# The residual add of a recurrent layer's feed-forward result: VectorE or GpSimd, and where a factor of one half is applied

## The chip, the cores and the metric

The kernel runs on one core of a Trainium2 chip. The metric is the device time of one execution in microseconds (us), taken as the median of several runs. Each engine works through its own queue in order: TensorE (PE, with its weight loads as PEld), VectorE (DVE), ScalarE (ACT), GpSimd (POOL) and SyncE (SP), which issues most of the transfers.

## The reference, cut to what matters

Four layers follow one another on an activation of 32 sequences x 64 positions x 256 features: a cross-attention layer (L0), two transformer blocks with self-attention, cross-attention and an MLP (L1, L2), and a recurrent layer (L3) in the manner of RWKV. The change is in the last lines of L3, its feed-forward part:

```python
x = x + att * g @ Wo.T
xn2 = _ln(x, ln2_w, ln2_b)
sx2 = _token_shift(xn2, state[:, i0])
xk = xn2 + sx2 * ffn_maa_k
xr = xn2 + sx2 * ffn_maa_r
rr = jax.nn.sigmoid(xr @ ffn_Wr.T)
kk = jnp.square(jax.nn.relu(xk @ ffn_Wk.T))
x = x + rr * (kk @ ffn_Wv.T)
return x
```

The sigmoid is computed as (1 + tanh(z / 2)) / 2. So the result is x + 0.5 * (1 + tanh) * (kk @ ffn_Wv.T), and the factor of one half can stand in the last step or in the weights ffn_Wv.

## The kernel before

The 2048 rows are held in SBUF in four groups (`xg[g]`, 128 partitions x 4 x 256). The recurrent layer works on eight slabs of 256 rows (`n` = 0 to 7; slab n is half u = n % 2 of group g = n // 2). For each slab `recurrent` returns three lists of small pieces:

- first: a layer norm (`norm`), the token-shift mixes (`mixed`, L681, VectorE, two inputs in SBUF; `mix`, which evacuates px on VectorE in L718 and adds xn on GpSimd in L721), the projections to receptance, key, value and gate (pr, pk, pv, pg), and the decay.
- second: `spread` (L754, a transfer that copies the values of a slab out of DRAM to 128 partitions), `outer` and `read` (L814, VectorE products of 128x2048), `scan` (L829, VectorE), `over_keys`, the group norm (L847 to L866) and the output projection with Wo (pwo, L875), which is added to x in L216.
- third: the second layer norm, the mixes xk and xr, and the three feed-forward products. `done_r` puts the tanh into the tile rr (ScalarE, L909). `done_v` finishes the slab: L914 computes (rr + 1) * pfv with pfv in PSUM, L915 multiplies by 0.5 and adds the rows of x, and L916 sends the result to DRAM through SP.

Each piece has a due time (FIRST, SECOND and THIRD plus the slab's number; ENDS shifts the last slabs), and `emit` writes all pieces out in the order of these times. The eight slabs therefore overlap: while slab n finishes, slabs n + 3 and n + 4 are in their second and first lists, and the rest of L2's MLP is interleaved with the first slabs. From that order the tile framework works out the final order on each engine when the program is built: among the instructions that its own timing estimate holds to be ready, it takes the one written first. Each engine then runs its queue in order, with semaphore waits for data and for buffers.

The weights of L3 that are needed late (Wg, Wo, ffn_Wk, ffn_Wr, ffn_Wv) are loaded through SP by `load_w` when the pool of the recurrent layer is set up; `ffn_Wv` is a tile of 128 x 2 x 256.

Of the kernel before, what the change touches and what calls it, by code (L numbers as in the profile page):

```python
# [34 lines left out]
ALU = mybir.AluOpType  # L35
# [5 lines left out]
NG = 4  # L41
# [51 lines left out]
def emit(*timed_lists):  # L93
    for _, piece in sorted((p for ps in timed_lists for p in ps), key=lambda p: p[0]):
        piece()
# [3 lines left out]
def tile_xattn_stack(ctx: ExitStack, tc: tile.TileContext, a: dict, out: bass.AP):  # L99
    nc = tc.nc  # L100
# [18 lines left out]
    xg = [const.tile([P, NT, E], FP, name=f"x{g}") for g in range(NG)]  # L119
# [11 lines left out]
    def vec(name, i=0):  # L131
        c = VEC[name] + i
        return vecs[:, c : c + 1]
# [89 lines left out]
    def ring(pool, name, shape, n, fill):  # L223

        tiles = [pool.tile(shape, FP, name=f"{name}{i}", bufs=1) for i in range(n)]
        for t in tiles:
            fill(t)
        turn, busy = [0], [False] * n

        def take():  # L230
            turn[0] += 1
            i = turn[0] % n
            assert not busy[i], name
            busy[i] = True

            def done():
                busy[i] = False

            return tiles[i], done

        return take
# [389 lines left out]
    def recurrent(n, pool, c3):  # L631

        g, u = n // 2, n % 2
# [277 lines left out]
        def done_v(ps):  # L911
            js = slice(2 * u, 2 * u + 2)
            rr = st["rr"]
            nc.vector.scalar_tensor_tensor(rr, rr, 1.0, ps, ALU.add, ALU.mult)  # L914
            nc.vector.scalar_tensor_tensor(rr, rr, 0.5, xg[g][:, js, :], ALU.mult, ALU.add)  # L915
            nc.sync.dma_start(out_rows[g][:, js, :], rr)  # L916

        def ff_norm():
# [2 lines left out]
        third = [(0.5, ff_norm), (0.0, ff_mix), (1.7, ff_key)]  # L921
        third += to_rows(lambda: st["xr"], "ffn_Wr", done_r, "fr")
        third += to_rows(lambda: st["kk"], "ffn_Wv", done_v, "fv")
        return first, second, third


    wts, c3 = {}, {}

    def load_to(pool, name, shape, src):
        c3[name] = pool.tile(shape, FP, name=name, bufs=1)  # L930
        nc.sync.dma_start(c3[name], src)
# [207 lines left out]
    with tc.tile_pool(name="r", bufs=2, reuse_waits="tile") as pool:  # L1139
        def load(name, shape, src):  # L1140
            load_to(pool, name, shape, src)

        def load_w(*names):
            for n in names:
                load(n, [P, 2, E], a["w3"][W3[n]].rearrange("(c p) n -> p c n", p=P))

        def hold(tag, bufs=2, shape=None):
            pool.tile(shape or [P, 2, RR], FP, tag=tag, name=f"hold_{tag}", bufs=bufs)

        def shifted_ring(name):  # L1150

            c3[name] = ring(pool, name, [P, 2, RB, S], 2, lambda t: nc.gpsimd.memset(t[:, :, :, 0], 0.0))

        hold("fx")
        hold("dfx")
        hold("x5", 3)
        hold("nx", 1)
        shifted_ring("wsh")
        hold("xk")
        hold("xr")  # L1160
        hold("kk")
        hold("x")
        hold("rr", 2, [P, 2, E])
        hold("dx")
        shifted_ring("vsh")
        hold("ta", 1, [P, RR + S])
        hold("vT")
        hold("rT")
        hold("tb", 1, [XM, RR])
        hold("rk", 1)  # L1170
        hold("dT", 1, [64, RR])
        selu = c3["selu"] = pool.tile([P, 2, P], FP, name="selu", bufs=1)
        load_w("Wg", "Wo", "ffn_Wk", "ffn_Wr", "ffn_Wv")
        load("s0", [P, 2, RS, B], a["s0"])
        hold("gt")
        hold("at")
        hold("sq", 1)
        shifted_ring("ksh")
        hold("nfx", 1)
        for c in range(2):  # L1180
            nc.vector.tensor_scalar(selu[:, c], c3["sel"][:, c], vec("L3_faaaa", c), None, ALU.mult)
        gnh = c3["gnh"] = pool.tile([P, 4], FP, name="gnh", bufs=1)
        for i, n in enumerate(("L3_gn_w", "L3_gn_b")):
            nc.vector.tensor_scalar(
                gnh[:, 2 * i : 2 * i + 2], vecs[:, VEC[n] : VEC[n] + 2], 0.5, None, ALU.mult
            )

        plan = [late]
        for n in range(2 * NG):
            for pieces, at, end in zip(recurrent(n, pool, c3), (FIRST, SECOND, THIRD), ENDS):  # L1190
                shift = end[n - 2 * NG] if n >= 2 * NG - len(end) else 0.0
                plan.append([(n + t + shift, piece) for t, (_, piece) in zip(at, pieces, strict=True)])
        emit(*plan)
# [78 lines left out]
```

## Time and profile before

| | us |
|---|---|
| median of 3 runs | 1058.6 |
| lowest and highest run | 1056.49 and 1059.2 |
| the profiled execution | 1057.36 |
| its span on the core | 1055.6 |
| busy: TensorE / VectorE | 963.1 / 741.4 |
| busy: ScalarE / GpSimd | 553.4 / 554.9 |

The span runs from the first to the last instruction that the profile shows; the profiled execution's time contains some 1.8 us more. The granted TensorE clock was 0.974 of full speed in the mean. A row of a timeline gives the start and duration in us, the engine, the line of the kernel, the operation, what it writes and reads, and in brackets how long the engine was idle before it and which instruction ended that. Rows of one kind that follow each other are merged ("x2"), so a duration can be that of several instructions.

### The profile page before, as it was taken

The page shows a single profiled execution, that of the slowest core. Times are in us where ns is not written, and L with a number is a line of the kernel's source. Part 1 is how long each engine was busy: PE and PEld are TensorE (multiplying, and loading weights), DVE is VectorE, ACT ScalarE, POOL GpSimd, SP SyncE. Part 2 cuts the span into 40 slices and gives each one's busy share as a digit, 9 for nine tenths or more (in the row PEclk, how much of TensorE's full clock was granted, in tenths as well). Part 3 has the DMA queues.
Part 4 walks back from the last instruction along what each step waited for, and adds up shares of the span by engine and source line. Part 5 has one row for each costly group of instructions (what it writes and reads, how often), then busy time and mean ns, then how long its engine had stood idle before and what let it go on. Part 6 is the DMA issues. An engine that isn't in the chain of part 4 may idle for free.

```text
span 1055.6 us, 25954 instructions
## 1 busy us (share of the span) xinstructions
PE 963.1 (91%) x10636; PEld 776.0 (74%) x10636; DVE 741.4 (70%) x1415; ACT 553.4 (52%) x1279; POOL 554.9 (53%) x584
## 2 busy tenths in 40 slices
PE   8999999998999999989999999997979989989757
PEld 4887787776788987967777778875857777666546
DVE  5863778787875646567777865337588786899984
ACT  4744756454466445654554575533545566355244
POOL 4343998798874347578688875130224431243300
PEclk9999999999999999999999999998989999999889
DMA  9300111111101000141101110021321304223401
GB/s 302 112 22 21 42 27 42 42 28 27 32 2 47 1 16 7 58 135 38 41 23 27 27 52 22 11 67 26 92 65 28 90 12 102 70 52 72 100 1 40
DMA packets 45945, 53.36 MB, mean 51 GB/s; under 512 B 16146, under 2 KB 40068, under 8 KB 43780
## 3 DMA queue, kind: packets, MB, share of 16 engines
q1 hardware_dynamic: 40292, 49.60, 17.6%
q10 hardware_dynamic: 5536, 2.12, 0.8%
q8 instruction: 84, 1.38, 0.5%
q14 instruction: 33, 0.27, 0.1%
HBM read 38.83 MB, written 4.21 MB: 41 GB/s over the span
## 4 chain that ended last, share of the span: by engine, by line
PE 43%; DVE 27%; POOL 14%; ACT 7%; issue 3%; DMA 3%; SPq 2%; ACTq 0%; DVEq 0%; POOLq 0%
DVE vb_r L829 7%; PE pf_L2m L205 4%; PE pfo_L1m L205 3%; PE pfo_L2m L613 3%; DVE vb_r L814 3%; POOL s_L2s L481 2%; PE pf_L1m L205 2%; POOL s_L1c L481 2%; POOL s_L2s L485 2%; PE pr L330 2%; SPq L421 2%; DVE x L216 1%; PE pwo_r L875 1%; POOL s_L1c L485 1%; PE pk_r L210 1%
## 5 line engine op out<-in xcount | busy, mean ns | idle before, releaser
L721 POOL TENSOR_TENSOR x_r<-x_r,xn_r 128x512 f32<-128x512 f32 x40 | 60.6, 1530 | 143.1 <-DVE x_r L718 131.8
L829 DVE TENSOR_TENSOR_SCAN vb_r<-wsh,vb_r 128x512 f32<-128x512 f32 x64 | 76.5, 1262 | 14.2 <-ACT wsh L725 14.2
L613 PE MATMUL pfo_L2m<-w_L,hT_L2m 128*128 128x256 f32 x256 | 61.2, 383 | 0.1
L205 PE MATMUL pfo_L1m<-w_L,hT_L1m 128*128 128x256 f32 x384 | 56.0, 292 | 4.7 <-DVE hT_L1m L605 2.1
L205 PE MATMUL pf_L2m<-lnT_L2m,w_L 128*128 128x256 f32 x384 | 55.2, 294 | 2.1 <-ACT hT_L2m L599 2.1
L205 PEld LDWEIGHTS pfo_L1m<-w_L,hT_L1m 128*128 128x128 f32 x384 | 50.5, 195 | 7.8 <-DVE hT_L1m L605 2.9
L205 PEld LDWEIGHTS pf_L2m<-lnT_L2m,w_L 128*128 128x128 f32 x384 | 49.0, 190 | 5.6 <-ACT hT_L2m L599 2.7
L613 PEld LDWEIGHTS pfo_L2m<-w_L,hT_L2m 128*128 128x128 f32 x256 | 47.0, 190 | 7.9 <-issue 1.3
L481 POOL TENSOR_TENSOR s_L2s<-s_L2s,n 128x512 f32<-128x512 f32 x32 | 41.5, 1314 | 20.9 <-DVE s_L2s L476 15.1
L205 PE MATMUL pf_L1m<-lnT_L1m,w_L 128*128 128x256 f32 x384 | 51.6, 287 | 0.1
L481 POOL TENSOR_TENSOR s_L1s<-s_L1s,n 128x512 f32<-128x512 f32 x32 | 40.5, 1282 | 19.7 <-DVE s_L1s L476 19.6
L481 POOL TENSOR_TENSOR s_L1c<-s_L1c,n_L1c 128x512 f32<-128x512 f32 x32 | 41.0, 1302 | 17.0 <-DVE s_L1c L476 16.8
L481 POOL TENSOR_TENSOR s_L2c<-s_L2c,n_L2c 128x512 f32<-128x512 f32 x32 | 40.5, 1286 | 17.6 <-DVE s_L2c L476 17.6
L205 PEld LDWEIGHTS pf_L1m<-lnT_L1m,w_L 128*128 128x128 f32 x384 | 47.8, 191 | 2.0 <-issue 1.2
L605 DVE TENSOR_TENSOR hT_L1m<-hf_L1m,hT_L1m 128x512 fp32r<-128x512 f32 x32 | 29.2, 916 | 24.6 <-POOL hT_L1m L604 24.6
L604 POOL TENSOR_SCALAR hT_L1m<-hf_L1m 128x512 fp32r<-128x512 f32 x32 | 21.4, 671 | 45.6 <-ACT hf_L1m L599 39.6
L599 ACT ACTIVATE hf_L1m<-pf_L1m,b_L 128x256 f32<-128x256 f32 x64 | 26.8, 473 | 29.1 <-PE pf_L1m L205 26.3
L599 ACT ACTIVATE hT_L2m<-pf_L2m,b_L 128x256 f32<-128x256 f32 x64 | 26.6, 472 | 29.0 <-PE pf_L2m L205 28.9
L718 DVE SCALAR_TENSOR_TENSOR x_r<-px_r,vecs,sx_r 128x256 f32<-128x256 f32 x80 | 33.5, 475 | 9.2 <-PE px_r L150 9.2
L300 ACT ACTIVATE att<-pe,nmx 128x256 f32<-128x256 f32 x64 | 29.6, 478 | 19.1 <-DVE nmx L298 16.8
L814 DVE TENSOR_TENSOR vb_r<-vb_r,rT_r 128x2048 f32<-128x2048 f32 x16 | 38.5, 2413 | 0.0
L150 PE MATMUL pa_r<-vb_r,sel 128*32 128x256 f32 x256 | 20.4, 447 | 19.2 <-DVE vb_r L814 19.2
(383 smaller groups left out, 2973.6 us busy)
## 6 DMA issues: line engine op xcount, KB each, us to landing
vb_r<-vd_r SPq DMA_DIRECT2D x16, 1024.0 KB
raw_w_L<-in_L_w_dram SPq DMA_DIRECT2D x3, 1024.0 KB
y<-in_y_dram SPq DMA_DIRECT2D x8, 256.0 KB
x<-in_x_dram SPq DMA_DIRECT2D x8, 256.0 KB
ctxT_L1c<-in_yT_dram SPq DMA_DIRECT2D x4, 512.0 KB
kbd<-kT_L1s SPq DMA_DIRECT2D x64, 32.0 KB
kbd<-kT_L1c SPq DMA_DIRECT2D x64, 32.0 KB
kbd<-kT_L2s SPq DMA_DIRECT2D x64, 32.0 KB
```

What stands on the lines that cost most here:

```text
L205: nc.tensor.matmul(ps, sta[x], mov[y], start=(at == 0), stop=(at == n - 1))
L300: nc.scalar.activation(att[:, 2 * h + c, :], pe[:, c, :], AF.Exp, bias=nmx[:, h, c : c + 1], accum_out=rs[:, h, c : c + 1],)
L481: nc.gpsimd.tensor_tensor(s[:, r], s[:, r], n(j).unsqueeze(1).broadcast_to([P, 8, S]), ALU.add)
L485: nc.gpsimd.tensor_tensor(s[:, r], s[:, r], mx[:, hs].unsqueeze(2).broadcast_to([P, 8, S]), ALU.subtract)
L599: nc.scalar.activation(raw[:, i], ps[:, i], AF.Gelu_apprx_tanh, bias=w()["b1"][:, 2 * f2 + i : 2 * f2 + i + 1])
L604: nc.gpsimd.tensor_scalar(h[:, 0], raw, 1.0, 0.0, ALU.mult, ALU.add)
L605: nc.vector.tensor_tensor(h[:, 1], raw, h[:, 0], ALU.subtract)
L613: nc.tensor.matmul(st["ps"][:, v], st["h"][:, f, rows], w2[:, f], start=(f == 0), stop=(f == 7))
L718: nc.vector.scalar_tensor_tensor(d[:, c], banks[m][:, c], vec("L3_maa_stack", 2 * m + c), sx_("x", c), ALU.add, ALU.mult)
L721: nc.gpsimd.tensor_tensor(d, d, st["x"], ALU.add)
L814: nc.vector.tensor_tensor(v, v, x.unsqueeze(1).broadcast_to([P, 4, 2 * RR]), ALU.mult)
L829: nc.vector.tensor_tensor_scan(v[:, d], flat(st["wsh"]), v[:, d], 0.0, ALU.mult, ALU.add)
```

## The change

The add of the rows (L915) becomes a plain tensor-tensor add without the factor. In slabs 0 to 6 it is issued on GpSimd, in slab 7 on VectorE. The factor of one half goes into the weights ffn_Wv: after they are loaded, one GpSimd instruction multiplies the tile by 0.5 in place. L914 and L916 stay as they are, on VectorE and SP.

```diff
         def done_v(ps):
             js = slice(2 * u, 2 * u + 2)
             rr = st["rr"]
+
             nc.vector.scalar_tensor_tensor(rr, rr, 1.0, ps, ALU.add, ALU.mult)
-            nc.vector.scalar_tensor_tensor(rr, rr, 0.5, xg[g][:, js, :], ALU.mult, ALU.add)
+            (nc.vector if n == 2 * NG - 1 else nc.gpsimd).tensor_tensor(rr, rr, xg[g][:, js, :], ALU.add)
             nc.sync.dma_start(out_rows[g][:, js, :], rr)
...
         load_w("Wg", "Wo", "ffn_Wk", "ffn_Wr", "ffn_Wv")
+        nc.gpsimd.tensor_scalar(c3["ffn_Wv"], c3["ffn_Wv"], 0.5, 0.0, ALU.mult, ALU.add)
         load("s0", [P, 2, RS, B], a["s0"])
```

## The prediction

> **What bounds the kernel now.** I read the page first, then the recurrent part in stages (busy time by window), then the chain of waits in order of time, and last the rows of VectorE and GpSimd around every execution of L915, the line that changes engine.
>
> ```profile
> PE 963.1 (91%) x10636; PEld 776.0 (74%) x10636; DVE 741.4 (70%) x1415; ACT 553.4 (52%) x1279; POOL 554.9 (53%) x584
> ...
> 910.00:950.00 40.00, 33.89 (x211) 25.07 (x210) 35.79 (x52) 22.55 (x44) 17.84 (x13) 0.99 0.33 80
> 950.00:990.00 40.00, 34.94 (x181) 24.15 (x180) 38.79 (x52) 14.67 (x30) 12.51 (x10) 0.88 0.38 89
> 990.00:1033.00 43.00, 29.35 (x168) 21.46 (x167) 36.64 (x52) 19.94 (x37) 5.81 (x7) 0.88 0.11 30
> 1033.00:1056.00 23.00, 16.48 (x81) 13.35 (x79) 9.08 (x20) 8.26 (x16) 1.26 (x4) 0.98 0.10 34
> ```
>
> In a window's row the columns are the window, its length, then the busy time of TensorE, its weight loads, VectorE, ScalarE and GpSimd. Over the whole span TensorE is the fullest. In the stretch where the changed code runs it is another matter: from 910 to 990 VectorE is busy 35.8 and 38.8 of 40 us, GpSimd 17.8 and 12.5. From 1033 on nobody is full: a chain through all engines ends the kernel. The chain of waits agrees: from 896 to 1017 it runs mostly through VectorE's scans (L829) and products (L814), and after that through TensorE.
>
> L915 runs eight times, at 871.63, 894.84, 957.86, 994.28, 1028.05, 1038.67, 1046.49 and 1051.66 (slabs 0 to 7). What follows it on VectorE decides what its removal is worth. Slab 1, then 2, then 3, and what GpSimd does near 2 and 3 (start, duration, engine, line; in brackets the idle time ahead and who ended it):
>
> ```profile
> 894.84 0.69 DVE L915 SCALAR_TENSOR_TENSOR rr_r<-rr_r,x 128x512 f32<-128x512 f32 x1
> 896.41 9.03 DVE L829 TENSOR_TENSOR_SCAN vb_r<-wsh,vb_r 128x512 f32<-128x512 f32 x8 [0.88 <-ACT wsh L725]
> ...
> 952.58 0.67 DVE L914 SCALAR_TENSOR_TENSOR rr_r<-rr_r,pfv_r 128x512 f32<-128x512 f32 x1
> 954.75 2.40 DVE L681 SCALAR_TENSOR_TENSOR xm_r<-sx_r,vecs,xn_r 128x256 f32<-128x256 f32 x2
> 957.86 0.68 DVE L915 SCALAR_TENSOR_TENSOR rr_r<-rr_r,x 128x512 f32<-128x512 f32 x1
> 959.62 0.69 DVE L216 TENSOR_TENSOR x<-x,pwo_r 128x512 f32<-128x512 f32 x1 [0.49 <-PE pwo_r L875]
> 994.28 0.67 DVE L915 SCALAR_TENSOR_TENSOR rr_r<-rr_r,x 128x512 f32<-128x512 f32 x1
> 995.59 0.69 DVE L765 TENSOR_TENSOR rk_r<-pk_r,rT_r 128x512 f32<-128x512 f32 x1 [0.64 <-ACT ksh L725]
> 996.20 4.49 DVE L814 TENSOR_TENSOR vb_r<-vb_r,ksh 128x2048 f32<-128x2048 f32 x2
> ...
> 954.18 2.68 POOL L721 TENSOR_TENSOR x_r<-x_r,xn_r 128x512 f32<-128x512 f32 x2 [9.98 <-DVE x_r L718]
> 994.53 1.57 POOL L721 TENSOR_TENSOR x_r<-x_r,xn_r 128x512 f32<-128x512 f32 x1 [2.23 <-DVE x_r L718]
> ...
> 879.47 0.88 DVE L681 SCALAR_TENSOR_TENSOR xm_r<-sx_r,vecs,xn_r 128x256 f32<-128x256 f32 x2
> ```
>
> Two things are to be seen. VectorE idles shortly after L915 in each of the three (0.88, 0.49 and 0.64 us), for TensorE or ScalarE. And the xm pair took 2.40 us at 954.75, beside a GpSimd add, against 0.88 at 879.47, where GpSimd was idle: the two engines get in each other's way.
>
> **Removed: seven of the eight L915.** Their durations are 1.18, 0.69, 0.68, 0.67 and three of 0.69, together 5.29 us of VectorE. On the path I count nothing. Slab 0: the next instruction (L865, at 872.74) waits for ScalarE's L862 until 872.34 and could start some 0.3 us earlier, but its result goes to a product (L875, pwo) that stands behind px in TensorE's queue until 875.35. Slab 1: the scan waits for ScalarE anyway. Slab 2: L847 moves up 0.6 us, then L216 waits for TensorE as before. Slab 3: L765 waits for ScalarE. Slabs 4 to 6: VectorE is idle afterwards for 1.54, 3.77 and 3.76 us. If this cover were gone, the four adds ahead of the tail would give 1.18 + 0.69 + 0.68 + 0.67 = 3.22 us, no more.
>
> **Added: seven adds on GpSimd.** The same shape with two inputs in SBUF is L721: 1.28 us alone (the row at 876.50), 1.53 in the mean of forty, 3.16 at the worst (989.14). So 7 x 1.28 = 9.0 us of an engine that is half idle; what counts is whom an add meets. Near rows give the price of a meeting from both sides. The xm pair lost 2.40 - 0.88 = 1.52 us; an instruction that reads PSUM lost nothing (L718, 953.17 to 954.82, ran beside a GpSimd add at its usual 1.65 for four). So the bounds are 0 and 1.5 us for each add; below nothing only by the removed 3.22.
>
> [...]
>
> Slab by slab from the rows. Slab 0: L914 ends at 871.59, GpSimd's pair of x_r adds at 872.26; the new add fills 872.26 to 873.54 and touches L866 at 873.52: 0. Slab 1: L914 ends at 894.81; with 0.14 us from VectorE to GpSimd the add lies at 894.95 to 896.23, and the scan starts at 896.41: 0, by 0.18 us only. Slab 2: L914 ends at 953.25. Ahead of the x_r pair, the add runs 953.4 to 954.7 and pushes the pair, and xm behind it, by 0.5; behind the pair it runs from 956.9 and meets L866 (two SBUF inputs, at 957.07, on the path to pwo and pk): 0 to 1.28. I take 0.5, the row that fits the order of L914 and the pair in time. Slab 3: ahead of the x_r add (994.53), the two end at about 996.3, 0.1 after the L814 on the path wants to start; behind it the add ends at 997.1, 0.9 after. I take 0.5. Slabs 4 to 6: GpSimd does nothing from 1024.5 to 1035.85 and after 1043.1, and 6 us are free after 1037: 0. Sum: +1.0 us.
>
> **The last slab** keeps VectorE, a plain add for one with a factor: 0.69 us either way (L216, a plain add of this size, takes 0.69): 0.
>
> **The halved weights.** One GpSimd instruction on 128x512 f32, like L604 and L390: 0.62 to 0.67 us, once. It waits for ffn_Wv's transfer, issued at 654.38; the windows by the microsecond show the DMA share at 0.83 until 657 and 0.00 from 657 to 658, so the data is there at about 657. Around it:
>
> ```profile
> 659.16 2.05 POOL L485 TENSOR_TENSOR s_L2c<-s_L2c,mx_L2c 128x512 f32<-128x512 f32 x2
> 671.58 0.19 POOL L167 TENSOR_SCALAR rstd_r<-mv_r 128x2 f32<-128x2 f32 x1 [10.36 <-DVE mv_L2m L165]
> ```
>
> GpSimd idles 10.36 us after 661.2, and 6.2 us after 678.4: 0. Queued in front of the softmax adds at 656.71, it would hold them to about 657.7, some 1 us, less where TensorE has other work. First use of the weights is at 855, so nothing else waits.
>
> **The transfers out** (L916) start 0.6 to 0.9 us later. SP works in order: behind slab 0's stands the spread of a later slab (L754, at 873.68), whose data is used from 884.96; behind slabs 1 and 2 nothing for 17 and 6 us. At the end slab 6's result leaves at about 1048, slab 7's as before at 1052.4: 0.
>
> Against the profiled execution (1057.36, span 1055.6) the sum gives 1058.4. The median of the runs shown is 1058.6, 1.2 above the profiled one; I carry the difference over: 1058.6 + 1.0 = 1059.6.
>
> **The rivals.** The order on each engine is worked out when the program is built, from due times and the builder's estimate of what is ready: eight other instructions lie between L914 and L915 in slab 2. So the change can move neighbours.
>
> Faster: the freed VectorE time is filled. For it: 38.8 of 40 us busy from 950 to 990, and L915 itself held up GpSimd's add at 994.53 (1.57 for 1.28, 0.3 us). If the order comes out so that scans and products close up, all counts: 3.22 + 0.3 = 3.5, 1055.1. Against it: the idle times after L915. It decides if the waits of 0.49 and 0.64 us vanish.
>
> [...]
>
> That the change removes no wait anybody has is the forecast itself.
>
> **How the numbers follow.** About 0.3% (3.2 us) is what a measurement of this kernel can tell from no change: 1055.4 to 1061.8. The forecast (its own range 1057.5 to 1061.8) gets 0.40, faster 0.25, slower 0.35; slower above faster since every meeting costs more (1.28) than an L915 returns (0.68). The range reaches beyond both rivals by about 1 to 1.5 us, for neighbours that the order moves: 1054.0 to 1066.5, with about 0.2 outside.
>
> **What would show it.** In the changed profile: seven adds on GpSimd of 1.3 to 1.6 us, VectorE down by 4 to 5 us in all, its busy share from 910 to 1033 barely changed, and the idle times after L914 in slabs 2 and 3 grown by what left. The halving stands between 661 and 684. Wrong if the scans beside an add are longer than 1.14 us each, if x_r adds are queued behind a waiting add, or if the rows before 850 have another order.

## The result and the profile after

| | median us | runs | range us | against before |
|---|---|---|---|---|
| before | 1059.19 | 19 | 1056.49 to 1063.54 | 1 |
| the change | 1062.78 | 19 | 1058.23 to 1067.02 | 1.003, 95% interval 1.0015 to 1.0044 |

The change costs 1.6 to 4.7 us. Its profiled execution took 1064.17 us (span 1062.4, granted clock 0.969), 6.8 us more than that of before. The page's line of busy times (share of the span, number of instructions) reads:

```profile
PE 967.2 (91%) x10636; PEld 780.1 (73%) x10636; DVE 738.9 (70%) x1408; ACT 553.4 (52%) x1279; POOL 562.4 (53%) x592
```

VectorE has seven instructions fewer and GpSimd eight more, as the diff says. In the changed kernel the lines below the second list shift by one: the add is L916, the transfer out L917, the halving L1175; L914 has become L915.

The halving and the first four adds on GpSimd, from the timeline (start, duration, engine, line; idle time and releaser in brackets):

```profile
682.51 0.62 POOL L1175 TENSOR_SCALAR ffn_Wv<-ffn_Wv 128x512 f32<-128x512 f32 x1
688.74 0.22 POOL L665 TENSOR_TENSOR sx_r<-st,xn_r 128x8 f32<-128x8 f32 x1 [5.61 <-ACT sx_r L661]
...
877.88 1.31 POOL L916 TENSOR_TENSOR rr_r<-rr_r,x 128x512 f32<-128x512 f32 x1
...
900.56 1.27 POOL L916 TENSOR_TENSOR rr_r<-rr_r,x 128x512 f32<-128x512 f32 x1 [2.64 <-DVE rr_r L915]
...
959.77 1.27 POOL L916 TENSOR_TENSOR rr_r<-rr_r,x 128x512 f32<-128x512 f32 x1 [9.13 <-DVE rr_r L915]
961.00 2.67 POOL L721 TENSOR_TENSOR x_r<-x_r,xn_r 128x512 f32<-128x512 f32 x2
...
1000.46 1.27 POOL L916 TENSOR_TENSOR rr_r<-rr_r,x 128x512 f32<-128x512 f32 x1 [1.35 <-DVE rr_r L915]
1001.68 1.28 POOL L721 TENSOR_TENSOR x_r<-x_r,xn_r 128x512 f32<-128x512 f32 x1
```

The halving stands where GpSimd idles. Slab 2's add (959.77) stands ahead of the pair of x_r adds, slab 3's (1000.46) ahead of the single one. VectorE beside the adds of slabs 1, 2 and 3, and the last slab's add:

```profile
899.79 0.69 DVE L915 SCALAR_TENSOR_TENSOR rr_r<-rr_r,pfv_r 128x512 f32<-128x512 f32 x1 [0.17 <-PE pfv_r L875]
902.08 9.03 DVE L829 TENSOR_TENSOR_SCAN vb_r<-wsh,vb_r 128x512 f32<-128x512 f32 x8 [1.60 <-ACT wsh L725]
...
961.19 2.77 DVE L681 SCALAR_TENSOR_TENSOR xm_r<-sx_r,vecs,xn_r 128x256 f32<-128x256 f32 x2
...
966.43 0.69 DVE L216 TENSOR_TENSOR x<-x,pwo_r 128x512 f32<-128x512 f32 x1 [1.09 <-PE pwo_r L875]
...
1002.40 0.69 DVE L765 TENSOR_TENSOR rk_r<-pk_r,rT_r 128x512 f32<-128x512 f32 x1 [1.23 <-ACT ksh L725]
1003.00 4.48 DVE L814 TENSOR_TENSOR vb_r<-vb_r,ksh 128x2048 f32<-128x2048 f32 x2
...
1058.47 0.69 DVE L916 TENSOR_TENSOR rr_r<-rr_r,x 128x512 f32<-128x512 f32 x1
```

The scans at 902.08 take the same 9.03 us as before: slab 1's add ended at 901.83. The xm pair takes 2.77 us where it took 2.40. The idle times ahead of L216 and L765 have grown from 0.49 and 0.64 to 1.09 and 1.23.

**A measure that does not depend on the start.** Each slab has eight scans (L829). The first scan of one slab to the first of the next is a step; the eight slabs give seven steps and an end. Mind the overlap: the scan that follows slab 1's add is that of the fifth slab. In us:

| steps from slab to slab | 1st-2nd | 2nd-3rd | 3rd-4th | 4th-5th | 5th-6th | 6th-7th | 7th-8th | to the end |
|---|---|---|---|---|---|---|---|---|
| before | 40.80 | 41.05 | 46.95 | 44.48 | 37.65 | 35.94 | 31.79 | 53.78 |
| the change | 42.19 | 41.76 | 46.95 | 44.48 | 38.42 | 36.31 | 31.78 | 53.79 |

Four of the eight agree within 0.01 us. Two steps near slabs 1 and 2 differ by 0.77 and 0.37. The first two (+2.10 together) and the time ahead of the first scan (+3.57) make up the rest of the 6.8. The busy times by window show the two steps, before and after (window, length, busy time of TensorE, its weight loads, VectorE, ScalarE, GpSimd, then clock, share of the DMA engines and GB/s):

```profile
896.41:934.06 37.65, 35.13 (x210) 25.97 (x209) 33.44 (x49) 15.00 (x31) 14.91 (x11) 1.00 0.30 71
934.06:970.00 35.94, 30.34 (x185) 22.15 (x183) 34.73 (x46) 17.33 (x37) 9.77 (x10) 0.95 0.32 75
```

```profile
902.08:940.50 38.42, 35.06 (x210) 26.01 (x209) 33.95 (x49) 15.00 (x31) 13.50 (x11) 1.00 0.28 70
940.50:976.82 36.32, 30.36 (x186) 22.15 (x183) 34.51 (x46) 17.34 (x38) 11.00 (x11) 0.95 0.32 74
```

In the longer step 5th-6th TensorE is busy for 35.1 us both times: it has no more work, it stands still 0.8 us longer. Its rows show where. Before:

```profile
913.17 1.13 PE L210 MATMUL pr_r<-x_r,Wr 128*128 128x256 f32 x4 [1.03 <-POOL x_r L721]
914.32 1.13 PE L859 MATMUL pgv_r<-sq_r,avg 128*128 128x256 f32 x4
915.28 1.03 PE L210 MATMUL pr_r<-x_r,Wr 128*128 128x256 f32 x4
...
923.80 1.99 PE L210 MATMUL pk_r<-x_r,Wk 128*128 128x256 f32 x8
```

After:

```profile
919.98 1.13 PE L859 MATMUL pgv_r<-sq_r,avg 128*128 128x256 f32 x4 [2.18 <-DVE x L216]
920.95 1.89 PE L210 MATMUL pr_r<-x_r,Wr 128*128 128x256 f32 x8
...
930.53 1.99 PE L210 MATMUL pk_r<-x_r,Wk 128*128 128x256 f32 x8
```

The builder has put pgv ahead of all of pr. What pgv waits for is not its input: sq_r has been there for over 20 us. It is the PSUM bank, the buffer for its output. In kernel.py pfo_L2m and pgv both take the bank with the tag "pc", of which there is one, and L216 on VectorE is the last to read pfo_L2m from it; it ends at 919.93, pgv starts at 919.98:

```profile
897.52 0.62 ACT L853 ACTIVATE sq_r<-at_r 128x512 f32<-128x512 f32 x1
...
919.26 0.67 DVE L216 TENSOR_TENSOR x<-x,pfo_L2m 128x512 f32<-128x512 f32 x1
```

Before, half of pr (1.15 us from its start to pgv's) ran while pgv had to wait for the bank anyway (L216 ended at 914.26, pgv started at 914.32); now TensorE stands still for 2.18 us ahead of pgv and does that half afterwards. pgv starts 17.9 us after the scan in both, and from there to the end of pk, without a gap, it takes 11.48 us before and 12.54 after. From pk hangs ksh (ScalarE, L725), L765 and L814. Two neighbours moved as well: the second half of pfr stands behind pwo instead of ahead of it, and on VectorE two evacuations of px stand behind both pairs of statistics (L164) of the next norms instead of between them, and the xm pair behind three of the four aggregates (L165) instead of one. Apart from these and the moved instructions themselves, the order on every engine is that of before, to the end.

### The profile page after: what moved, and what is told of

Its sections match the earlier page's. It is cut to its first block, busy times and chain, and to the rows that moved or that the text cites. A ratio compares the mean times of both kernels' runs of the same rounds, so it can differ in the third digit from the quotient of the medians.

```text
span 1062.4 us, 25968 instructions
## 1 busy us (share of the span) xinstructions
PE 967.2 (91%) x10636; PEld 780.1 (73%) x10636; DVE 738.9 (70%) x1408; ACT 553.4 (52%) x1279; POOL 562.4 (53%) x592
## 4 chain that ended last, share of the span: by engine, by line
PE 44%; DVE 25%; POOL 14%; ACT 7%; DMA 4%; issue 3%; SPq 2%; DVEq 0%; ACTq 0%; POOLq 0%
DVE vb_r L829 7%; PE pf_L2m L205 4%; PE pfo_L2m L613 3%; DVE vb_r L814 3%; PE pfo_L1m L205 2%; POOL s_L2s L481 2%; PE pf_L1m L205 2%; POOL s_L1c L481 2%; POOL s_L2s L485 2%; SPq L421 2%; PE pr L330 1%; PE pk_r L210 1%; PE pwo_r L875 1%; DVE x L216 1%; POOL s_L1c L485 1%
## 5 line engine op out<-in xcount | busy, mean ns | idle before, releaser
L829 DVE TENSOR_TENSOR_SCAN vb_r<-wsh,vb_r 128x512 f32<-128x512 f32 x64 | 76.4, 1261 | 15.1 <-ACT wsh L725 15.1
L814 DVE TENSOR_TENSOR vb_r<-vb_r,rT_r 128x2048 f32<-128x2048 f32 x16 | 38.5, 2412 | 0.0
```

The source lines that it names most:

```text
L814: nc.vector.tensor_tensor(v, v, x.unsqueeze(1).broadcast_to([P, 4, 2 * RR]), ALU.mult)
L829: nc.vector.tensor_tensor_scan(v[:, d], flat(st["wsh"]), v[:, d], 0.0, ALU.mult, ALU.add)
```

## The experiments

Every ratio is of the runs of that kernel to the runs of the kernel before on the same chip, with its 95% interval. Steps of all of them (the two that matter), in us:

| kernel | ratio | 5th-6th | 6th-7th |
|---|---|---|---|
| before, again | 1.0002 (0.9987 to 1.0016) | 37.66 | 35.93 |
| the change, again | 1.0024 (1.0005 to 1.0043) | 40.12 | 36.31 |
| halving only | 0.9983 (0.9964 to 1.0003) | 37.66 | 35.93 |
| move only | 1.0017 (1.0000 to 1.0033) | 38.42 | 36.31 |
| slab 1 only | 1.0008 (0.9992 to 1.0023) | 38.43 | 35.93 |
| all but slab 1 | 0.9993 (0.9971 to 1.0014) | 37.65 | 36.31 |
| all but slabs 1 and 2 | 0.9972 (0.9951 to 0.9993) | 37.66 | 35.93 |
| rows added twice | 1.0050 (1.0033 to 1.0068) | 39.38 | 38.81 |
| pfr put back | 1.0014 (0.9995 to 1.0034) | 40.21 | 36.32 |
| add behind the pair | 1.0041 (1.0011 to 1.0070) | 40.20 | 36.95 |
| pfr put back, slab 2 on VectorE | 1.0024 (1.0002 to 1.0045) | 40.20 | 35.94 |
| no add in slab 1 | 1.0030 (1.0005 to 1.0055) | 40.12 | 35.94 |

**Both kernels again, without an edit.**

> The kernel before, unchanged, once more. Both profiles, of before and of the change, already differ by 4.0 us at 654 us (the issue of the transfer of ffn_Wv: 654.4 against 658.4), ahead of every edited instruction and with the same order on every engine. Theory A (the adds meet VectorE, and everything ahead of 682 us is variation from one execution to the next): the ratio is 1.000 within 0.0015, and this profile's issue of ffn_Wv may lie anywhere from 653 to 660. Theory C (the 4 us belong to the changed program): this profile has it at 654.4 within 0.5.

> The changed kernel, unchanged, once more. Theory A: ratio 1.001 to 1.003; from the first scan (L829) to the end of the span about 1.0 to 1.5 us more than in the kernel before (332.5 there), where the first profile of the change showed 3.2 because TensorE's granted clock was lower from 735 to 818. Theory C: ratio 1.003, and the issue of ffn_Wv again at 658.4.

Before against itself is 1.0002, the change 1.0024. The steps of before return within 0.01 us from the third on; ahead of the first scan the same program took 3.3 us more (726.4 against 723.1). So that part of a profile varies from run to run, and only the steps can be compared, best those from the third on. The change's step 5th-6th came out at 40.12 this time instead of 38.42; why is below.

**The halving alone, and the move alone.** All eight adds plain on VectorE with the halved weights; and the adds moved with the half put into a scale of ScalarE's L904 in place of the halving:

```diff
-            (nc.vector if n == 2 * NG - 1 else nc.gpsimd).tensor_tensor(rr, rr, xg[g][:, js, :], ALU.add)
+            nc.vector.tensor_tensor(rr, rr, xg[g][:, js, :], ALU.add)
```

```diff
-            nc.scalar.activation(kk, kk, AF.Square)
+            nc.scalar.activation(kk, kk, AF.Square, scale=0.5 ** 0.5)
...
-        nc.gpsimd.tensor_scalar(c3["ffn_Wv"], c3["ffn_Wv"], 0.5, 0.0, ALU.mult, ALU.add)
```

> The halving of the weights alone: ffn_Wv is halved on GpSimd, and all eight adds of the rows are plain adds on VectorE. Theory A (the adds on GpSimd cost, the halving nothing): ratio 1.000 within 0.001, the halving of 0.62 us stands in an idle stretch of GpSimd of 5 us or more, and the plain adds take 0.69. Theory B (the halving costs, by its place in GpSimd's queue or by the wait of TensorE on it): ratio 1.002 to 1.003, like the whole change.

> The move alone: the adds of slabs 0 to 6 on GpSimd, no halving of the weights; the factor of one half lies in the scale of ScalarE's Square of kk (scale 0.7071), an instruction that is there anyway. Theory A: ratio as for the whole change, 1.001 to 1.003. Theory B (the halving costs): ratio 1.000 within 0.001.

The halving alone has every step of before from the third on; the move alone has the two longer steps of the change. The cost is the move's, the halving's is nothing.

**Which slab.** The adds are on GpSimd in slab 1 alone; in all but slab 1 and the last; in all but slabs 1, 2 and the last:

```diff
+            (nc.gpsimd if n == 1 else nc.vector).tensor_tensor(rr, rr, xg[g][:, js, :], ALU.add)
+            (nc.vector if n in (1, 2 * NG - 1) else nc.gpsimd).tensor_tensor(rr, rr, xg[g][:, js, :], ALU.add)
+            (nc.vector if n in (1, 2, 2 * NG - 1) else nc.gpsimd).tensor_tensor(rr, rr, xg[g][:, js, :], ALU.add)
```

> As the change, but only slab 1's add is on GpSimd; the others are plain adds on VectorE, and the weights are halved. In this program VectorE's and TensorE's queues have the changed order near slab 1 (pgv ahead of pr, two px evacuations behind two statistics, pwo ahead of pfr). Theory D (that order costs): from the start of slab 4's scans to slab 5's 38.42 us as in the change, against 37.65 before; all later steps as before (35.94, 31.79, 53.77); ratio 1.0007 plus what lower clocks add. Theory A (the meetings of the engines cost): 37.65, since slab 1's add ends ahead of the scan; ratio 1.000.

> As the change, but slab 1's add is on VectorE. All other instructions have the order of the kernel before. Theory A: the step from slab 5's scans to slab 6's is 36.31 us as in the change (35.94 before), for the add of slab 2 that goes ahead of the x_r pair; theory D: the step from slab 4's scans to slab 5's is back at 37.65. Both together: ratio 1.000 to 1.001, 0.37 us over before.

> As the change, but the adds of slabs 1 and 2 are on VectorE; slabs 0, 3, 4, 5 and 6 stay on GpSimd. Both theories together: every step between scans as before (37.65, 35.94, 31.79, 53.77), ratio 1.000 within 0.0015. If the halving or the adds of the last slabs cost anything, the last step (slab 7's scans to the end) is over 53.8 or the ratio 1.001 and more.

The two terms come apart cleanly: slab 1 alone gives 38.43 and leaves the next step at 35.93; all but slab 1 gives 37.65 and 36.31; without both every step from the third on is that of before. The adds of slabs 0, 3, 4, 5 and 6 cost nothing. VectorE's rows at the end of the longer step tell how it is passed on. Before, L765 starts without a wait behind mv_r:

```profile
926.65 0.21 DVE L165 BATCH_NORM_AGGREGATE mv_r<-stats_r 128x2 f32<-128x6 f32 x2
926.78 0.65 DVE L765 TENSOR_TENSOR rk_r<-pk_r,rT_r 128x512 f32<-128x512 f32 x1
```

With slab 1's add alone on GpSimd it waits for ksh, and so for pk:

```profile
932.52 0.69 DVE L765 TENSOR_TENSOR rk_r<-pk_r,rT_r 128x512 f32<-128x512 f32 x1 [0.26 <-ACT ksh L725]
```

pk ends 1.06 us later against pgv (12.54 - 11.48), and from pk to the next slab's scan 7.98 us pass instead of 8.27, since VectorE no longer makes anyone wait there: 1.06 - 0.29 = 0.77.

**The adds of slabs 0 to 3 doubled.** The rows are added twice there, so these rows of the result hold them twice:

```diff
+            if n in (0, 1, 2, 3):
+                nc.gpsimd.tensor_tensor(rr, rr, xg[g][:, js, :], ALU.add)
```

> The change with slab 0 to 3's GpSimd add done twice (the rows of x are added twice there, so that the result of these slabs differs from the reference). Theory A (lock and queue): the second add of slab 1 runs into the scans and costs 1.0 us there, that of slab 2 pushes the x_r pair and xm by 1.27 more, that of slab 3 holds the product of slab 7 (L814) by up to 1.2; slab 0's is hidden. About 2.5 to 3.5 us over the change, ratio 1.005 to 1.007. If GpSimd work of this size is hidden here, the ratio is that of the change, 1.002 to 1.003.

Steps 5th-6th, 6th-7th and 7th-8th are 0.96, 2.50 and 1.06 longer than in the change. Slab 1's second add reaches into the scans, which take longer:

```profile
900.86 9.97 DVE L829 TENSOR_TENSOR_SCAN vb_r<-wsh,vb_r 128x512 f32<-128x512 f32 x8 [1.60 <-ACT wsh L725]
...
900.68 1.27 POOL L918 TENSOR_TENSOR rr_r<-rr_r,x 128x512 f32<-128x512 f32 x1
```

The scans take 9.97 us for 9.03. What the expectation calls a lock shows in the runs as this longer duration beside a GpSimd add, and as no more than that. The change escapes it by the 0.25 us between its add and the scan. Slab 3's second add (1005.16) meets L814, which takes 5.53 us for 4.48. Slab 2's second add pushes the second x_r add back, and this one meets the L866 pair. The step grows by more than the 1.27 us expected there, because the clock joins in (three rows of instructions, then two windows):

```profile
963.36 1.44 POOL L721 TENSOR_TENSOR x_r<-x_r,xn_r 128x512 f32<-128x512 f32 x1
963.61 1.87 DVE L866 SCALAR_TENSOR_TENSOR at_r<-at_r,gnh,gt_r 128x256 f32<-128x256 f32 x2
965.14 3.49 PE L875 MATMUL pwo_r<-Wo,at_r 128*128 128x256 f32 x8 [2.21 <-DVE at_r L866]
...
961.38:964.79 3.41, 1.54 (x7) 0.75 (x5) 3.41 (x3) 0.60 (x1) 3.41 (x3) 1.00 0.67 164
964.79:968.20 3.41, 3.06 (x7) 2.52 (x8) 1.29 (x3) 0.00 (x0) 0.01 (x1) 0.50 0.09 31
```

L866 takes 1.0 us more (0.87 in the change), and pwo, which waits for it, falls into a window at half clock and takes 1.5 us more (1.99 in the change): 2.5 together. So an add on GpSimd did cost about a microsecond where it met a two-input instruction of the chain (0.94 us for the scans, 1.05 for L814, 1.0 for L866). In the change none of the adds of slabs 1 to 3 did: slab 2's ends at 961.04, ahead of xm at 961.19, and costs by its place in GpSimd's queue, ahead of the x_r pair.

**Order or add?** The last four kernels. The first gives the second half of pfr in slab 2 precedence, which puts pfr and VectorE's order back; the second has this edit and queues slab 2's add behind the pair of x_r adds; the third has it too, with slab 2's add on VectorE; the fourth is the halving alone with slab 1's add left out:

```diff
+                if name == "fr" and n == 2 and v == 1:
+                    with tc.high_priority():
+                        part(v)
...
+            with tc.issue_after(marks["x"].ins) if n == 2 else contextlib.nullcontext():
...
+            (nc.vector if n in (2, 2 * NG - 1) else nc.gpsimd).tensor_tensor(rr, rr, xg[g][:, js, :], ALU.add)
...
+            if n != 1:
+                nc.vector.tensor_tensor(rr, rr, xg[g][:, js, :], ALU.add)
```

> All of the change is there, but the second half of the pfr product of one slab (L875) is given precedence, so that VectorE's order is again that of the kernel before (px evacuations ahead of stats_r) and TensorE has pfr complete ahead of pwo. Slab 1's add stays on GpSimd. Order theory: the step from the fifth slab's first scan to the sixth's (L829) goes from the change's 38.42 us back to 37.65, the next one stays at 36.31 (slab 2's add is still ahead of the x_r pair), time 0.4 us above the kernel before. Rival (slab 1's add itself costs the 0.77): 38.4 stays.

> As the version with the order put back, and slab 2's add is queued on GpSimd behind the pair of x_r adds instead of ahead of it; no other instruction moves. Lock theory: the pair and xm start 0.4 us earlier, but the add now starts as the pair ends, 0.2 us ahead of L866, and holds it for some 1.0 us on the way to pwo: the step from the sixth to the seventh slab's scan becomes 36.9 us (35.94 before, 36.31 in the change). Rival (only GpSimd's queue matters, the meeting costs nothing): 35.94, and every step as before.

> As the version with the order put back, and slab 2's add is on VectorE again; slabs 0, 1, 3, 4, 5 and 6 keep theirs on GpSimd. If the two terms (order 0.77, queue 0.37) are all that the change costs: steps 37.65 and 35.94, every step between two scans within 0.05 us of the kernel before, and the time that of the kernel before within 0.1%. If GpSimd's adds cost anything elsewhere: one step longer, or a time 2 to 3 us above before.

> All adds on VectorE (plain), the weights halved, and slab 1's add left out altogether, so that this slab's rows lack the residual; the order on VectorE and TensorE is then that of the change near the fifth slab. Order theory: the step from the fifth to the sixth slab's scan is 38.4 us although GpSimd has no add at all; the others as before (35.94 next). Rival (slab 1's add on GpSimd costs): 37.65.

*Slab 2* came out as expected. Behind the pair the add meets L866 (L869 in this file), and the step is 36.95 (36.9 expected); on VectorE it is 35.94:

```profile
961.37 2.40 DVE L682 SCALAR_TENSOR_TENSOR xm_r<-sx_r,vecs,xn_r 128x256 f32<-128x256 f32 x2
963.69 1.87 DVE L869 SCALAR_TENSOR_TENSOR at_r<-at_r,gnh,gt_r 128x256 f32<-128x256 f32 x2
...
960.80 2.67 POOL L722 TENSOR_TENSOR x_r<-x_r,xn_r 128x512 f32<-128x512 f32 x2 [9.99 <-DVE x_r L719]
963.44 1.44 POOL L927 TENSOR_TENSOR rr_r<-rr_r,x 128x512 f32<-128x512 f32 x1
```

xm is back at 2.40, but L866 takes 1.87 us instead of 0.87: the add, from 963.44 to 964.88, runs beside it, and this meeting costs the pair 1.0 us.

*Slab 1* did not: neither 37.65 nor 38.4, but 40.20 and, without any add, 40.12. My idea that pfr and VectorE's order were the operative part fell; in all four kernels pr still stands behind pgv. The step that no account had is in the clock. The windows of the kernel without an add in slab 1, cut at the changes of the granted clock:

```profile
912.98:916.39 3.41, 1.23 (x6) 0.78 (x5) 2.50 (x3) 1.90 (x3) 1.97 (x2) 1.00 0.16 44
916.39:919.81 3.42, 3.42 (x10) 2.46 (x8) 0.80 (x3) 2.55 (x4) 0.00 (x0) 0.50 0.67 170
```

In the traces of before and of the change every stretch between two changes of the granted clock lasts a multiple of 3.41 us (at half clock 3.41, 6.83 or 10.24), and the windows here are cut on that grid. In the first window TensorE is busy for 1.23 us, because it waits for pgv; in the next the clock is 0.50, and pr takes 3.50 us instead of 1.89:

```profile
915.53 1.25 PE L859 MATMUL pgv_r<-sq_r,avg 128*128 128x256 f32 x4 [2.18 <-DVE x L216]
916.58 3.50 PE L210 MATMUL pr_r<-x_r,Wr 128*128 128x256 f32 x8
```

With half of pr ahead of pgv (here the kernel with all but slabs 1 and 2), the same window holds 2.36 us of work, and the clock stays at 1.00:

```profile
913.58:916.99 3.41, 2.36 (x10) 1.43 (x9) 2.53 (x3) 1.87 (x3) 2.00 (x2) 1.00 0.15 41
916.99:920.41 3.42, 3.42 (x22) 2.23 (x24) 0.76 (x2) 3.08 (x5) 0.00 (x0) 1.00 0.67 181
```

In the profiled run of the change the grid lay otherwise, and the same wait was shared by two windows:

```profile
914.87:918.29 3.42, 2.94 (x18) 2.33 (x16) 3.42 (x3) 2.49 (x5) 3.42 (x2) 1.00 0.00 0
918.29:921.70 3.41, 1.72 (x8) 1.54 (x9) 1.64 (x2) 2.30 (x4) 1.12 (x2) 1.00 0.26 75
921.70:925.11 3.41, 3.41 (x22) 2.20 (x24) 1.65 (x5) 2.21 (x4) 0.00 (x0) 1.00 0.83 211
```

With 2.94 and 1.72 us of TensorE work in the two windows the clock stayed at 1.00, and the step cost 0.77 only. So the changed order cost 0.77 us (38.42) or 2.47 us (40.12) in the two profiles of the change, in which the grid fell differently on the wait. With pfr and VectorE's order put back and the clock halved it costs 2.55 (40.20), so these neighbours do not add to it. Over the fourteen profiled runs (before, the change and these twelve) this holds without exception: in the five with half of pr ahead of pgv the step is 37.65 or 37.66; in five of the nine with pr behind pgv the clock halved there (40.12 to 40.21; pr took 3.46 to 3.52 us), and in the other four it did not (pr 1.89), 38.42 and 38.43 and, with the adds doubled, 39.38. (In that last one it halved a window earlier, at 913.59, for work ahead of pgv, where pst took 1.83 us for 1.16, and TensorE still waited 0.77 us for the bank.) The five and the four differ in the first two steps as well, which took 81.5 to 81.7 us together in the five and 83.8 to 84.0 in the four. The two profiles of the change also lie differently on the grid: the fifth slab's first scan starts 1.7 us after an edge of it in the second (one of the five, and the same without an add in slab 1), 0.9 us in the first (one of the four).

The times point the same way, though single intervals overlap. The four other runs with half of pr ahead of pgv (before again and three variants) have ratios of 0.9972 to 1.0002, the nine with pr behind it 1.0008 to 1.0050. The kernel without an add in slab 1 has no add on GpSimd at all and is as slow as the change (1.0030 against 1.003): in step 5th-6th the order is the cause, not the add.

## Why the prediction was right, and where it was not

The time forecast was 1059.6 and came out at 1062.78, inside the range of 1054.0 to 1066.5 and 3.2 us above the forecast. It lies outside the forecast's own 1057.5 to 1061.8. Of an add's two possible costs, its place in GpSimd's queue and a meeting with VectorE, only the first was at work, in slab 2, for 0.37 us. That the range held is due to its width, drawn for rivals and for an order that moves, and so in part luck; the sum itself was too small. No run shows the 1.28 us of VectorE for every meeting that the chances and the upper end of the range are drawn from: the meetings on the chain measured 0.94 us (scans), 1.05 (L814) and 1.0 (L866), in other runs than the change, where the adds of slabs 1 to 3 met nothing of the chain. Step by step:

- **Slab 2, +0.5: right, 0.37.** The add stands ahead of the x_r pair, pair and xm move back as described, L216 waits 1.09 us for pwo. The bound of 1.28 for the other order measured 1.01 (36.95 - 35.94).
- **Slab 3, +0.5: 0.** The two adds were put to end 0.1 us after L814 could start. They end at 1002.96, L814 starts at 1003.00, behind a wait for ksh; the step is 31.78 for 31.79. The mechanism had no room, by 0.04 us.
- **Slab 0, slabs 4 to 6, the last slab, the halving, the transfers: 0, as forecast.** The halving stands at 682.51, in the stretch named.
- **Slab 1, 0: the step that failed.** The add did keep clear of the scan (901.83 against 902.08). But "the scan waits for ScalarE anyway" looked only at the instruction that follows L915 on VectorE. In every kernel with slab 1's add off VectorE's queue pr stands behind pgv some 20 us later, in every one with it there half of pr stands ahead: 0.77 us, or 2.47 with the halved clock. That the builder's estimate of what is ready shifted by the 0.69 us is the likely reason; the estimate itself is not on record. The text had said that the order could move, and let it widen the range; the forecast had no term for it.
- **VectorE down by 4 to 5 us: 2.5** (741.4 to 738.9). Seven L915 left 5.29 us, but instructions beside the moved work grew, xm by 0.37 and L866 in slab 0 by 0.17 (1.04 for 0.87) among them. The rest lies in the layers ahead, which vary: the kernel before, run again, has 742.1.
- **The rivals.** The freed VectorE time was not filled: the waits of 0.49 and 0.64 us grew by 0.60 and 0.59. That the change is slower is not the price of a meeting: slab 1's add started 1.52 us ahead of the scans, slab 2's 1.42 ahead of xm, and both had ended by then (901.83 and 961.04). The price is real where adds do meet the chain, 0.94 to 1.05 us with the doubled adds.

The two terms give 0.77 + 0.37 = 1.14 us, or 2.47 + 0.37 = 2.84 where the clock halves; measured were 1.6 to 4.7 us, and 0.5 to 4.6 in the repeat. The profiles agree with that: from the first scan to the end the change took 335.7 and 335.1 us, before 332.4 and 332.1. The second profile of the change is over those of before by 2.6 and 2.9, and the 2.84 fit that. The first is over by 3.3 and 3.6: the 1.14, and 2.1 to 2.4 in its longer first two steps. How often each case comes in runs without a profile is not known, and so is whether the change makes the longer first steps more frequent (one of five profiles with half of pr ahead of pgv, four of nine with pr behind it): that stays open.

The rest of the 6.8 us between the two profiled runs lies where the programs are the same but for the halving, and was seen without the halving too: the first two steps are 2.1 us longer in five of the fourteen runs (the half-clock stretch at the first scans lasted 10.24 us in the first profile of the change, one of the five, and 6.83 in that of before, one of the others), one of them with the order of before.

No version here is clearly better than the kernel before. The adds of all slabs but 1 and 2 moved gave 0.9972 (0.9951 to 0.9993), yet its steps are those of before, so its trace does not explain a gain; the halving alone, with the same steps, gave 0.9983. All adds on GpSimd with half of pr ahead of pgv was not tried.

## What to carry to other kernels

Moving an instruction off a queue whose order a builder works out is also an edit of that order: compare the order on every engine, far behind the edit too, before pricing anything, and price a matmul that changes sides of a wait by what it filled. Look at the clock behind a wait as well: one order cost 0.77 us here, and 2.47 where it left TensorE 1.23 us of work in one window of 3.41 and the clock halved in the next. Compare traces by steps between recurring instructions; here those from the third on repeat to 0.03 us where order, meetings and clock are the same, while whole runs differ by several us.

## What the runs showed of the hardware

The granted clock fell to half, in stretches of 3.41, 6.83 and 10.24 us, also after windows in which TensorE had been far from idle. In the traces of before and of the change, of the windows of 3.41 us that lie on the grid between 690 and 1052 us, every one at full clock with up to 1.40 us of TensorE work was followed by one at 0.50, and none with more than 1.57. In between both occurred: 1.44 us at 812.87 before, and the clock stayed at 1.00; 1.56 us at 696.42 in the change, and it fell. The windows of other runs shown above are in line with that: 1.23 us at 912.98 and 1.54 at 961.38 were followed by 0.50, 2.36 at 913.58 by 1.00.
